# Small tasks moved among the groups of an attention pipeline, and a split moved to another PSUM bank

## The chip, the cores and the metric

The kernel runs on one core of one Trainium2 chip. The metric is the device time of one execution in microseconds (us). The engines are TensorE (PE; PEld is its weight load), VectorE (DVE), ScalarE (ACT), GpSimd (POOL) and SyncE (SP, which issues most DMAs).

## What is computed

Per batch element b (8 of them, 1024 tokens of width 256) the reference computes, with six modulation rows from a small matmul:

```python
h = _layernorm(x) * (1 + ca) + sa
x = x + ga * attention(h)          # 16 heads of 64, softmax over 1024 keys, output projection
h = _layernorm(x) * (1 + cb) + sb
x = x + gb * experts(h)            # 8 experts, each takes its 512 best tokens of all 8192
```

The experts' scores are a softmax over `h @ router_w + router_b`. Everything is float32.

## The kernel before, in words

Attention fills most of the span. Its work is cut into 128 units: one batch element, one pair of heads and one half (512) of the queries. A unit has four groups, numbered over the whole kernel by `g`; group `g` belongs to unit `g // 4`, and `g % 4` is 0, 1, 2, 3 in what the text calls its first, second, third and fourth group. 64 groups are one batch element. Nothing schedules: the order is written out by hand under `manual_schedule`, each engine executes its instructions in that order, and the framework adds the waits.

Each group, in the main loop (L727 to L763), does in this order:

- loads queued for this group (`load`);
- VectorE: subtract the row maxima (L420) from two chunks of an earlier unit (the lag is six groups);
- TensorE: two score chunks of 128 keys (L361), each into one of the two tiles "s" of the pool `ps_s` (two PSUM banks each); ScalarE copies a chunk to SBUF (L370), VectorE folds it into the running maximum `top` (L375);
- `m1` tasks: a query or key projection (`qk_task`, L326) or a value projection (`v_task`, L343), each through the one-bank tile "mm" of `ps_m`, and copied out by ScalarE;
- `post` tasks, then ScalarE: exponentials of the two subtracted chunks (L423);
- TensorE: two values products (L432); POOL adds the exponentials up (L448, L451);
- in a fourth group: `max_turn` transposes `top` into a tile "s" (L382), and `split_max` reduces it to row maxima and splits these into three bf16 parts (L390 to L398);
- `pool` tasks, then `m2` tasks.

In the next unit's first group `max_rows` transposes the parts (L404) through "mm"; in its second group `max_spread` (L417) spreads them over the partitions. The tile "mm" has one buffer, so all small tasks pass through it one after another.

The small tasks around the change are these:

- `ln_task` (L311): the norm of the next batch's inputs, two token tiles at a time: `ln_load`, `ln_stats` (VectorE, L116 and L117), `ln_norm` (POOL, L106 to L276), `ln_out`. Before, `ln_out` of every batch but the first turns by 16 ordinary matmul instructions of 64 columns (L300), and VectorE scales and shifts both halves (L305). For the first batch it turns by four transposes (L288), two for each half k of the width, and ScalarE scales and shifts a half (L291) before the next half is turned.
- `out_load`, `out_proj` (L542), `out_add`, `out_norm` (POOL, L565 to L567): the output projection of one token tile and the second norm.
- `out_turn` (L579), `out_route` (L594), `out_exp` (ScalarE, L609), `out_score` (VectorE, L616 to L620), `out_store`: the router for a pair of token tiles.

Where they stand, before, is given by `free_slot`: `ln_out`, `out_proj` and `out_turn` each take a fourth group of their own, behind the split; `out_route` takes a group that is neither a first nor a fourth. `split_max` keeps its small intermediate values in the tile "s" that it reduces:

```python
nm = tt[:, :2, :8]
```

After attention come the last batch's projection and router (L766 to L818), the choice of tokens (L876 to L952) and the experts (L1052 on).

Of the kernel before, what the change touches and what calls it, by code (L numbers as in the profile page):

```python
# [28 lines left out]
F32 = mybir.dt.float32  # L29
BF16 = mybir.dt.bfloat16  # L30
I32 = mybir.dt.int32
AF = mybir.ActivationFunctionType
ALU = mybir.AluOpType
# [4 lines left out]
P = 128  # L38
# [4 lines left out]
def adaln_block(  # L43
# [15 lines left out]
    nc = tc.nc  # L59
    B, S, D = x.shape  # L60
    H, _, _, N = w_qkv.shape
    E, _, F = w1.shape
    K = 512
    KC = D // P
    NT = S // P
# [7 lines left out]
    scale = 1.0 / N**0.5  # L73
# [4 lines left out]
    ident = const.tile([P, P], F32, name="ident")  # L78
# [17 lines left out]
    modT = const.tile([P, 2 * KC, B], F32, name="modT")  # L96
# [36 lines left out]
    ps_m = attn.enter_context(tc.tile_pool(name="ps_m", bufs=1, space=PSUM))  # L133
# [35 lines left out]
    for i in range(2):  # L169
        t = work.tile([P, NT // 2, D], F32, tag="p", name=f"x_first{i}", bufs=PB)  # L170
# [65 lines left out]
    hTs, mods, qks, vs, oTs = {}, {}, {}, {}, {}  # L236
# [4 lines left out]
    def at(g, where, f, *args):  # L241
        steps.setdefault((g, where), []).append((f, args))
# [8 lines left out]
    def bank(shape, name, start=False):  # L251

        if start:
            return ps_s.tile(shape, F32, tag="s", name=name)
        return ps_m.tile(shape, F32, tag="mm", name=name)
# [24 lines left out]
    def ln_out(b, t):  # L280
        if t == 0:
            hTs[b] = work.tile([P, KC, S], F32, tag="hT", name=f"hT{b}")
        xt = ln_x.pop((b, t))[0]
        pt = bank([P, KC, 2 * P], f"ptx{b}_{t}", (b, t) in ((0, 0), (0, 1)))
        if b == 0:
            for k in range(KC):
                for i in range(2):
                    nc.tensor.transpose(  # L288
                        pt[:, k, i * P : (i + 1) * P], xt[:, i, k * P : (k + 1) * P], ident
                    )  # L290
                nc.scalar.activation(  # L291
                    hTs[b][:, k, 2 * t * P : (2 * t + 2) * P], pt[:, k, :], AF.Identity,
                    bias=modT[:, k, b : b + 1], scale=modT[:, KC + k, b : b + 1],
                )
            return
        for k in range(KC):
            for i in range(2):
                for m in range(2):
                    c0 = k * P + m * N
                    nc.tensor.matmul(  # L300
                        pt[m * N : (m + 1) * N, k, i * P : (i + 1) * P],
                        xt[:, i, c0 : c0 + N], ident, start=True, stop=True,
                    )
        for k in range(KC):
            nc.vector.tensor_scalar(  # L305
                hTs[b][:, k, 2 * t * P : (2 * t + 2) * P], pt[:, k, :],
                modT[:, KC + k, b : b + 1], modT[:, k, b : b + 1],
                op0=ALU.mult, op1=ALU.add,
            )

    def ln_task(b, t, g):  # L311
        at(g - 4, "load", ln_load, b, t)
        at(g - 2, "post", ln_stats, b, t)
        at(g - 1, "pool", ln_norm, b, t)
        at(g, "m2", ln_out, b, t)
# [67 lines left out]
                    turned[u][:, 4 * j + t, :], top[:, j, t * P : (t + 1) * P], ident  # L383
                )

    def split_max(u):

        tt = turned.pop(u)
        nm = tt[:, :2, :8]
        nc.vector.tensor_reduce(nm[:, 0, :], tt, AX.X, ALU.max, negate=True)  # L390
        part = [
            parts_of[u % 2][:, :, :, i].rearrange("p t j -> p j t") for i in range(3)
        ]
        whole, rest = (nm[:, i, :].rearrange("p (j t) -> p j t", j=2) for i in range(2))
        nc.vector.tensor_copy(part[0], whole)
        nc.vector.tensor_sub(rest, whole, part[0])
        nc.vector.tensor_copy(part[1], rest)
        nc.vector.tensor_sub(part[2], rest, part[1])  # L398
# [171 lines left out]
    def out_turn(pool, b, t, tag="mm"):  # L570

        n = f"{b}_{t}"
        pt = pool.tile([P, 2, KC, P], F32, tag=tag, name=f"pth{n}")
        for i in range(2):
            h2 = o_h[b, t + i]
            for k in range(KC):
                for m in range(2):
                    c0 = k * P + m * N
                    nc.tensor.matmul(  # L579
                        pt[m * N : (m + 1) * N, i, k, :], h2[:, c0 : c0 + N], ident,  # L580
                        start=True, stop=True,
                    )
        h2T = small.tile([P, 2, KC, P], F32, tag="h2T", name=f"h2T{n}", bufs=1)
        nc.scalar.copy(h2T, pt)
        o_x[b, t] = h2T
# [54 lines left out]
        )  # L640


    taken = set()

    def free_slot(g, behind=False):
        while g in taken or g % 4 == 0 or behind != (g % 4 == 3):
            g += 1
        taken.add(g)
        return g


    for t in range(NT // 2):
        at(-2 if t < 2 else -1, "m1", ln_out, 0, t)
        ln_task(1, t, free_slot(39 + 4 * t, True))
    for i, g in ((0, -2), (2, -2), (1, -1), (3, 0)):
        at(g, "m1", qk_task, 0, 0, i)
    for t, g in enumerate((-1, 0, 1)):
# [1 line left out]
    for b in range(B):  # L659
        for p in range(NP):  # L660
            P0 = 8 * (b * NP + p)
            for i, g in enumerate((-7, -6, -5, -2)):
                if P0:
                    at(P0 + g, "m1", qk_task, b, p, i)
            if p % 2 == 0:
                for t, g in enumerate((-9, -3, -1, 5)):
                    if P0 or g > 0:
                        at(P0 + g, "m1", v_task, b, p // 2, t)
            if (b, p) == (B - 1, NP - 1):
                continue  # L670

            at(P0 + 17, "load", den_load, b, p)
            at(P0 + 18, "post", den_inv, b, p)
            at(P0 + 19, "load", den_spread, b, p)
            at(P0 + 20, "pool", den_mul, b, p)
        if b + 1 < B:
            if b + 2 < B:
                for t in range(NT // 2):
                    ln_task(b + 2, t, free_slot(64 * (b + 1) + 39 + 4 * t, True))
            for t in range(NT):  # L680
                g = free_slot(64 * (b + 1) + 19 + 4 * t, True)
                at(g - 2, "load", out_load, b, t)
                at(g, "m2", out_proj, ps_m, b, t)
                at(g + 1, "pool", out_norm, b, t)
                if t % 2:
                    g = free_slot(g + 2, True)
                    at(g, "m2", out_turn, ps_m, b, t - 1)
                    g = free_slot(g + 1)
                    at(g, "m2", out_route, ps_m, b, t - 1)
                    at(g + 1, "post", out_exp, b, t - 1)  # L690
                    at(g + 2, "post", out_score, b, t - 1)
                    at(g + 3, "pool", out_store, b, t - 1)
    for u in range(NSU):
        at(4 * u + 4, "m1", max_rows, u)
        if u < NSU - 1:
# [8 lines left out]
    with tc.manual_schedule():  # L704
# [21 lines left out]
        g = -2  # L726
        while g < 4 * NSU + LAG or steps:  # L727
            u, gm = divmod(g, 4)
            run(g, "load")
            if gm == 1 and 0 < u <= NSU:  # L730
                max_spread(u - 1)
            u1, gm1 = divmod(g - LAG + 1, 4)
            late = [(u1, 2 * gm1 + i) for i in range(2) if 0 <= u1 < NSU]

            for uc in late[: 1 if gm == 3 else 2]:
                subtract(*uc)
            if 0 <= u < NSU:
                for c in (2 * gm, 2 * gm + 1):
                    scores_out(u, c, scores_mm(u, c))
            if gm == 3 and late:  # L740
                subtract(*late[1])
            run(g, "m1")
            run(g, "post")
            for uc in late:
                exp_of(*uc)
            u1, gm1 = divmod(g - LAG, 4)
            if 0 <= u1 < NSU:
                for c in (2 * gm1, 2 * gm1 + 1):
                    values_mm(u1, c)
                    if u1 == NSU - 1:  # L750
                        if c == 0:
                            pd_last = ps_s.tile([P, QH], F32, tag="s", name="pd_last")
                        den_mm(pd_last, probs.pop((u1, c)), start=(c == 0), stop=(c == NT - 1))
                if gm1 == 3:
                    values_out(u1)
                if u1 < NSU - 1:
                    add_up(u1, gm1)
            if gm == 3 and 0 <= u < NSU:
                max_turn(u)
                split_max(u)  # L760
            run(g, "pool")
            run(g, "m2")
            g += 1  # L763


        b = B - 1  # L766
# [82 lines left out]
    with tc.tile_pool(name="search", bufs=2) as se, tc.tile_pool(  # L849
        name="pos", bufs=1  # L850
    ) as po_, tc.tile_pool(name="se_ps", bufs=2, space=PSUM) as sps, tc.tile_pool(
        name="pos_ps", bufs=1, space=PSUM
    ) as pps:
        for dst, pattern, mult in (
# [3 lines left out]
            i = po_.tile(list(dst.shape), I32, name=f"i_{dst.name}")  # L858
# [29 lines left out]
        for s in range(15):  # L888
            bit = 28 - 2 * s
            cnt = se.tile([P, 3], F32, tag="cnt", name=f"cnt{s}")  # L890
            for k in range(3):
# [3 lines left out]
                    op0=ALU.is_ge, op1=ALU.add, accum_out=cnt[:, k : k + 1],  # L895
# [209 lines left out]
```

## Time and profile before

| | us |
|---|---|
| median of three runs | 3621.32 |
| lowest, highest run | 3620.8, 3622.61 |
| the profiled execution | 3623.01 |
| span of its trace | 3621.3 |

| line and engine | what | count | busy us | mean ns |
|---|---|---|---|---|
| L451 POOL | adding up exponentials | 762 | 1806.3 | 2370 |
| L420 DVE | subtracting maxima | 1024 | 1206.5 | 1209 |
| L423 ACT | exponentials | 1024 | 1041.8 | 1057 |
| L361 PE | scores | 4096 | 1024.6 | 612 |
| L432 PE | values product | 4096 | 968.2 | 593 |
| L382 PE | turn of the maxima | 1024 | 139.9 | 280 |
| L579 PE | router's turn | 512 | 39.1 | 296 |
| L300 PE | norms' turn | 448 | 30.6 | 279 |
| L305 DVE | scale and shift of the norms | 56 | 27.7 | 536 |
| L291 ACT | the same, first batch | 8 | 4.4 | 562 |

Busy time is the union of a group's intervals. A float32 matmul of the program stands in the trace as two instructions, a transpose as one. Matmuls overlap, so what a piece of TensorE's work takes of its chain is read from the start of its first matmul to the start of the next piece, not from the means.

### The profile page before, as it was taken

To read this page: it belongs to the slowest core of one execution; us is meant where nothing else is said; L and a number is where in the kernel's file an instruction comes from. 1 tells how busy PE (TensorE), PEld (TensorE's weight loads), DVE (VectorE), ACT (ScalarE), POOL (GpSimd) and SP (SyncE) were. 2 spreads that over 40 slices of the span, in tenths; PEclk is the share of its full clock that TensorE was granted. 3 is DMA by queue.
4 is the path that set the end of the run, shared out by engine and by line. 5 is a ranking of instruction groups with operands and counts; after the bars stand their busy time and mean duration, and the time that the engine had idled before them with its cause. 6 is when DMAs were issued, how large, how long until landed. Compare 5 with 4: busy or idle time off the path is not lost. (4 is left out here: it accounts for less than half of the span.)

```text
span 3621.3 us, 54202 instructions
## 1 busy us (share of the span) xinstructions
PE 3462.3 (96%) x20622; PEld 1457.6 (40%) x20622; DVE 2898.7 (80%) x3641; ACT 2436.6 (67%) x2988; POOL 2658.8 (73%) x1537
## 2 busy tenths in 40 slices
PE   7999999999999999999999999999999999982898
PEld 3333333343433443344433434334334344342565
DVE  4889888888888888888888888888888888857442
ACT  4777777777777777777777777777777777730111
POOL 1778778888788877977788788877788877851232
PEclk9999999999999999999999999999999999995999
DMA  4021013011121112111211112011301121133332
GB/s 77 13 42 31 25 32 66 30 45 45 58 52 35 49 52 64 31 39 51 58 48 44 40 44 62 30 52 48 67 29 45 45 59 48 51 87 121 94 100 41
DMA packets 189652, 185.39 MB, mean 51 GB/s; under 512 B 48952, under 2 KB 167240, under 8 KB 189264
## 3 DMA queue, kind: packets, MB, share of 16 engines
q1 hardware_dynamic: 170448, 159.50, 16.1%
q0 software_dynamic: 7168, 12.72, 1.7%
q10 hardware_dynamic: 11776, 9.71, 0.9%
q8 instruction: 162, 2.65, 0.3%
q14 instruction: 98, 0.80, 0.1%
HBM read 127.06 MB, written 63.21 MB: 53 GB/s over the span
## 5 line engine op out<-in xcount | busy, mean ns | idle before, releaser
L451 POOL TENSOR_TENSOR acc<-acc,p 128x1024 f32<-128x1024 f32 x762 | 1806.3, 2370 | 361.3 <-ACT p L423 328.2
L370 ACT COPY p<-s 128x1024 f32<-128x1024 f32 x1024 | 996.1, 1018 | 417.8 <-PE s L361 407.5
L420 DVE TENSOR_TENSOR p<-p,less 128x1024 f32<-128x1024 f32 x1024 | 1206.5, 1209 | 33.0 <-PE less L417 30.4
L375 DVE TENSOR_TENSOR top<-top,s 128x1024 f32<-128x1024 f32 x768 | 936.6, 1220 | 266.9 <-ACT p L370 226.6
L423 ACT ACTIVATE p<-p 128x1024 f32<-128x1024 f32 x1024 | 1041.8, 1057 | 73.8 <-DVE p L420 73.4
L361 PE MATMUL s<-qk,qk 64*128 64x512 f32 x4096 | 1024.6, 612 | 33.4 <-DVE parts L398 31.0
L432 PE MATMUL av<-p,v 128*64 128x512 f32 x4096 | 968.2, 593 | 1.8 <-ACT oT L441 1.8
L361 PEld LDWEIGHTS s<-qk,qk 64*128 64x128 f32 x4096 | 358.6, 186 | 525.6 <-issue 240.1
L326 PE MATMUL pq<-hT,wq 128*64 128x512 f32 x2048 | 498.7, 608 | 1.3 <-ACT v L348 0.7
L432 PEld LDWEIGHTS av<-p,v 128*64 128x64 f32 x4096 | 280.8, 137 | 461.8 <-issue 366.2
L448 POOL TENSOR_TENSOR acc<-p,p 128x1024 f32<-128x1024 f32 x127 | 301.7, 2376 | 183.3 <-ACT p L423 183.3
L326 PEld LDWEIGHTS pq<-hT,wq 128*64 128x64 f32 x2048 | 124.8, 136 | 341.8 <-issue 212.6
L343 PE MATMUL pv<-wq,hT 128*64 128x256 f32 x2048 | 251.0, 387 | 1.4 <-ACT qk L331 0.7
L1030 ACT ACTIVATE h<-ph,b_sb 128x512 f32<-128x512 f32 x64 | 44.0, 687 | 275.9 <-PE ph L1026 275.9
L390 DVE TENSOR_REDUCE tt<-tt 128x8 f32<-128x1024 f32 x128 | 157.4, 1230 | 68.3 <-PE tt L382 68.2
L542 PE MATMUL po<-wo,ot 128*64 128x256 f32 x1792 | 205.7, 382 | 0.0
L343 PEld LDWEIGHTS pv<-wq,hT 128*64 128x64 f32 x2048 | 136.3, 137 | 155.6 <-issue 66.3
L375 DVE TENSOR_TENSOR top<-p,s 128x1024 f32<-128x1024 f32 x128 | 155.7, 1217 | 29.9 <-ACT p L370 29.9
L382 PEld LDWEIGHTS tt<-ident,top 128*128 128x128 f32 x1024 | 109.6, 140 | 107.4 <-DVE top L375 107.4
L513 POOL TENSOR_TENSOR oT<-oT,rb 128x1024 f32<-128x1024 f32 x63 | 149.9, 2379 | 3.2 <-DMA rb<-rden_d 3.2
L542 PEld LDWEIGHTS po<-wo,ot 128*64 128x64 f32 x1792 | 123.5, 137 | 66.2 <-issue 9.4
L382 PE MATMUL tt<-ident,top 128*128 128x128 f32 x1024 | 139.9, 280 | 3.3 <-DVE top L375 3.3
(166 smaller groups left out, 2356.5 us busy)
## 6 DMA issues: line engine op xcount, KB each, us to landing
rb<-rden_d SPq DMA_DIRECT2D x128, 256.0 KB
oT_d<-oT SPq DMA_DIRECT2D x62, 512.0 KB
ot<-oT_d SPq DMA_DIRECT2D x56, 512.0 KB
rows_d<-row SPq DMA_DIRECT2D x64, 132.0 KB
rows_d<-gb_d SPq DMA_DIRECT2D x8, 1024.0 KB
w<-in_L_ffn_w_dram ACTq DMA_DIRECT2D x8, 1024.0 KB
w<-in_L_ffn_w_dram SPq DMA_DIRECT2D x8, 1024.0 KB
lnx<-in_L_attn_inputs_dram SPq DMA_DIRECT2D x28, 256.0 KB
```

The lines of the kernel that those rows point to most:

```text
L326: nc.tensor.matmul(pq[m * N : (m + 1) * N, :], wq_of(k, a, 2 * p + m), hTs[b][:, k, sl], start=(k == 0), stop=(k == KC - 1),)
L343: nc.tensor.matmul(pv[m * N : (m + 1) * N, i, :], hTs[b][:, k, t0 : t0 + N], wq_of(k, 2, 4 * g, 4), start=(k == 0), stop=(k == KC - 1),)
L361: nc.tensor.matmul(ps[:, j, :], kt[r, c * P : (c + 1) * P], qt[r, h * QB : (h + 1) * QB], start=True, stop=True,)
L370: nc.scalar.copy(probs[u, c], ps)
L375: nc.vector.tensor_tensor(tops[u], probs[u, 0] if c == 1 else tops[u], ps, ALU.max)
L382: nc.tensor.transpose(turned[u][:, 4 * j + t, :], top[:, j, t * P : (t + 1) * P], ident)
L420: nc.vector.tensor_tensor(probs[u, c], probs[u, c], less[u], ALU.add)
L423: nc.scalar.activation(probs[u, c], probs[u, c], AF.Exp)
L432: nc.tensor.matmul(avs[u][j * N : (j + 1) * N, :], v[:, c, hh * N : (hh + 1) * N], pT[:, j, :], start=(c == 0), stop=(c == NT - 1),)
L448: nc.gpsimd.tensor_tensor(sums[u], pts[0], pts[1], ALU.add)
L451: nc.gpsimd.tensor_tensor(sums[u], sums[u], pt, ALU.add)
L542: nc.tensor.matmul(po[m * N : (m + 1) * N, :], ot[:, p, m * N : (m + 1) * N], wo[:, p, :], start=(p == 0), stop=(p == NP - 1),)
```

## The change

It does four things. `ln_out` uses the first batch's form for all batches: transposes over the whole 128 x 128 array, and ScalarE for the output, half by half. `out_turn` uses transposes over the whole array as well. `split_max` gets a flag: where a projection follows in the same group, it works in the tile "s" as before, elsewhere in a tile "mm". And `free_slot` is gone: the norms' turns for batch b + 1 stand in the third groups of the first four units of batch b (groups 2, 6, 10, 14 of its 64; before, in its fourth groups 39, 43, 47, 51); the projections stand in fourth groups 19, 23, 31, 35, 43, 47, 55, 59 of the next batch's 64; the router's turn three groups after the second projection of a pair, which is a third group, its matmul six groups after, its exponentials, scores and stores seven, eight and nine groups after.

```diff
     def ln_out(b, t):
...
-        if b == 0:
-            for k in range(KC):
-                for i in range(2):
-                    nc.tensor.transpose(
-                        pt[:, k, i * P : (i + 1) * P], xt[:, i, k * P : (k + 1) * P], ident
-                    )
-                nc.scalar.activation(
-                    hTs[b][:, k, 2 * t * P : (2 * t + 2) * P], pt[:, k, :], AF.Identity,
-                    bias=modT[:, k, b : b + 1], scale=modT[:, KC + k, b : b + 1],
-                )
-            return
         for k in range(KC):
             for i in range(2):
-                for m in range(2):
-                    c0 = k * P + m * N
-                    nc.tensor.matmul(
-                        pt[m * N : (m + 1) * N, k, i * P : (i + 1) * P],
-                        xt[:, i, c0 : c0 + N], ident, start=True, stop=True,
-                    )
-        for k in range(KC):
-            nc.vector.tensor_scalar(
-                hTs[b][:, k, 2 * t * P : (2 * t + 2) * P], pt[:, k, :],
-                modT[:, KC + k, b : b + 1], modT[:, k, b : b + 1],
-                op0=ALU.mult, op1=ALU.add,
+                nc.tensor.transpose(
+                    pt[:, k, i * P : (i + 1) * P], xt[:, i, k * P : (k + 1) * P], ident
+                )
+            nc.scalar.activation(
+                hTs[b][:, k, 2 * t * P : (2 * t + 2) * P], pt[:, k, :], AF.Identity,
+                bias=modT[:, k, b : b + 1], scale=modT[:, KC + k, b : b + 1],
             )
...
-    def split_max(u):
+    def split_max(u, busy):
 
         tt = turned.pop(u)
-        nm = tt[:, :2, :8]
+
+        nm = tt[:, :2, :8] if busy else ps_m.tile([P, 2, 8], F32, tag="mm", name=f"nm{u}")
...
     def out_turn(pool, b, t, tag="mm"):
...
-                for m in range(2):
-                    c0 = k * P + m * N
-                    nc.tensor.matmul(
-                        pt[m * N : (m + 1) * N, i, k, :], h2[:, c0 : c0 + N], ident,
-                        start=True, stop=True,
-                    )
+                nc.tensor.transpose(pt[:, i, k, :], h2[:, k * P : (k + 1) * P], ident)
...
-    taken = set()
-
-    def free_slot(g, behind=False):
-        while g in taken or g % 4 == 0 or behind != (g % 4 == 3):
-            g += 1
-        taken.add(g)
-        return g
+
+    covered = set()
...
-        ln_task(1, t, free_slot(39 + 4 * t, True))
...
-            if b + 2 < B:
-                for t in range(NT // 2):
-                    ln_task(b + 2, t, free_slot(64 * (b + 1) + 39 + 4 * t, True))
+            for t in range(NT // 2):
+                ln_task(b + 1, t, 64 * b + 2 + 4 * t)
             for t in range(NT):
-                g = free_slot(64 * (b + 1) + 19 + 4 * t, True)
+                g = 64 * (b + 1) + 19 + 4 * (t + t // 2)
+                covered.add(g)
                 at(g - 2, "load", out_load, b, t)
                 at(g, "m2", out_proj, ps_m, b, t)
                 at(g + 1, "pool", out_norm, b, t)
                 if t % 2:
-                    g = free_slot(g + 2, True)
-                    at(g, "m2", out_turn, ps_m, b, t - 1)
-                    g = free_slot(g + 1)
-                    at(g, "m2", out_route, ps_m, b, t - 1)
-                    at(g + 1, "post", out_exp, b, t - 1)
-                    at(g + 2, "post", out_score, b, t - 1)
-                    at(g + 3, "pool", out_store, b, t - 1)
+                    at(g + 3, "m2", out_turn, ps_m, b, t - 1)
+                    at(g + 6, "m2", out_route, ps_m, b, t - 1)
+                    at(g + 7, "post", out_exp, b, t - 1)
+                    at(g + 8, "post", out_score, b, t - 1)
+                    at(g + 9, "pool", out_store, b, t - 1)
...
             if gm == 3 and 0 <= u < NSU:
                 max_turn(u)
-                split_max(u)
+                split_max(u, g in covered)
```

## The prediction

> **What bounds the kernel now.** I read the page first, then the waits, then the timeline of single units.
>
> ```profile
> PE 3462.3 (96%) x20622; PEld 1457.6 (40%) x20622; DVE 2898.7 (80%) x3641; ACT 2436.6 (67%) x2988; POOL 2658.8 (73%) x1537
> ```
>
> TensorE is busy for 96% of the span, the next engine for 80%. A busy TensorE proves little by itself, so I measured from the start of one piece of its work to the start of the next over all 512 groups. The pieces repeat to 0.01 us: two score chunks 1.91, a query/key task 1.77, a value task 1.78, a values product 1.82, a projection (L542) 3.60, the turn of the maxima (L382) 1.02, a turn of 16 small matmuls (L300, L579) 1.02. In the stretches between 36 and 3,200 us the clock column reads 1.00. So attention is one TensorE chain, and a microsecond put on it is a microsecond of time. Its only regular wait is in the waits view:
>
> ```profile
> PE s L361 <- DVE parts L398: 31.0, 70, 1.3
> ```
>
> Seventy of 128 units wait at their end. The timeline of a unit without small work at its end (columns: start, duration, engine, line, operation, tiles, idle before it):
>
> ```profile
> 83.08 1.09 PE L382 MATMUL tt<-ident,top 128*128 128x128 f32 x8
> ...
> 84.10 1.13 PE L361 MATMUL s<-qk,qk 64*128 64x512 f32 x4
> 84.21 1.23 DVE L390 TENSOR_REDUCE tt<-tt 128x8 f32<-128x1024 f32 x1 [0.74 <-PE tt L382]
> ...
> 86.14 0.19 DVE L398 TENSOR_TENSOR parts<-tt,parts 128x8 bf16<-128x8 f32 x1
> ...
> 86.48 1.13 PE L361 MATMUL s<-qk,qk 64*128 64x512 f32 x4 [1.25 <-DVE parts L398]
> 87.54 0.41 PE L404 MATMUL pn<-ident_b,parts 128*64 128x128 bf16 x8
> ```
>
> Let T be the start of L382 (83.08). The reduction ends at T+2.36, the split at T+3.25, and only 0.15 later, at T+3.40, does the second score chunk start, because the split works inside the score bank that this chunk needs. The row turn L404 starts at T+4.46. Now a unit with a turn of the next batch's norms at its end (T = 1106.22):
>
> ```profile
> 1107.24 1.09 PE L300 MATMUL ptx<-ident,lnx 128*64 128x128 f32 x16
> ...
> 1109.62 1.13 PE L361 MATMUL s<-qk,qk 64*128 64x512 f32 x4 [0.22 <-DVE parts L398]
> ...
> 1110.68 0.41 PE L404 MATMUL pn<-ident_b,parts 128*64 128x128 bf16 x8
> ```
>
> Again L404 starts at T+4.46: the 1.02 us turn lies wholly inside a wait that would be there anyway. That holds for all 28 turns L300 and all 27 turns L579 that are followed by a unit. With a projection there, L404 starts at T+6.54 and nothing waits.
>
> **What the change is worth, part by part.** The built order of the changed kernel leaves all 56 projections at units' ends, where the split stays in the score bank: nothing changes there, since the projection covers it (split done by T+5.03 at the latest, second chunk at T+5.59). The other 70 inner units (15 + 28 + 27) end with nothing.
>
> *Split in the small bank.* The second chunk now waits for the reduction: T+2.36 + 0.15 = T+2.51, and L404 follows 1.06 later at T+3.57 (the split's end plus 0.15, T+3.40, is earlier). Gain 4.46 - 3.57 = 0.89 per unit. No trace shows this release; its bounds are no gain (the split still holds the bank) and 1.06 (only the split's end holds L404). I take 0.89, from the row of the reduction that the built order names as what the chunk waits for. The small bank's last reader before it is a ScalarE copy that ended at 1105.20, 2.1 us before the reduction starts: no new wait. In six units it goes otherwise: the score operations of a batch's last pair (L616 to L620) now fall in a fourth group without a projection (the first units of batches 2 to 7, counted from 0). They push the reduction from T+1.13 to T+2.52 wherever they stand now, always under a projection. There the chunk starts at T+3.90 and L404 at T+4.96: 0.50 worse. Sum: -64 x 0.89 + 6 x 0.50 = **-54.0**.
>
> *Turns over the whole array, in third groups.* They now stand on the chain. Starts within L382 are 0.166 and then 0.109 apart, and 0.205 passes from the last to the next mode's matmul, so four transposes cost 0.166 + 2 x 0.109 + 0.205 = 0.59, against 1.02 for 16 matmuls. The router's turn (out_turn, all four, then one copy) costs that: 27 x 0.59 = **+15.9** (bounds 0.59 and the present 1.02). POOL ended its rows 9.2 us after the projection's start and the turn comes 19 us after it, so no wait.
>
> [...]
>
> *The next batch's norms.* Here the code, not the size, matters. The two halves (k) share one tile; ScalarE reads the first half before the second is turned, and the built order makes the second half's transposes wait for that ScalarE instruction. The first batch does so already, at the start of the trace:
>
> ```profile
> 24.65 0.44 PE L288 MATMUL ptx<-ident,x_first 128*128 128x128 f32 x2
> ...
> 25.26 0.56 ACT L291 ACTIVATE hT<-ptx,modT 128x256 f32<-128x256 f32 x1
> ...
> 25.88 0.44 PE L288 MATMUL ptx<-ident,x_first 128*128 128x128 f32 x2 [0.79 <-ACT hT L291]
> 26.35 0.56 ACT L291 ACTIVATE hT<-ptx,modT 128x256 f32<-128x256 f32 x1 [0.53 <-PE ptx L288]
> ```
>
> Half to half takes 1.22 us with an idle ScalarE. In a third group ScalarE is not idle. Such a group, from 1095.21:
>
> ```profile
> 1099.60 1.99 ACT L423 ACTIVATE p<-p 128x1024 f32<-128x1024 f32 x2
> ...
> 1100.71 1.99 PE L361 MATMUL s<-qk,qk 64*128 64x512 f32 x8
> ```
>
> Its values product ends 5.50 us after the group's start (1100.71), where the turn will be; the exponentials, queued ahead, end at 6.38. ScalarE overlaps successive instructions by 0.1, so the first half's output runs 6.28 to 6.84, the second half's transposes start 0.05 later at 6.90, and the next scores at 6.90 + 0.166 + 0.205 = 7.27. Queued behind the waiting transposes on TensorE is everything: the scores and all after. So such a turn costs 7.27 - 5.50 = 1.77, not 0.59. In five of them out_exp (L609) stands ahead of the exponentials and moves them by 0.38 (849.36 in a group that starts at 844.59): 2.15. Bounds: 0.59 (no wait) and 2.15 everywhere; the rows favour 1.77. 22 x 1.77 + 5 x 2.15 = **+49.7**. The second half's ScalarE output ends near 7.95, before copy 6 can start (7.27 + 1.23). VectorE loses 56 x 0.54 (L305), which covered nothing. The statistics (1.08) move to first groups, where by the rows VectorE ends the maximum that frees the sixth chunk's bank at T+12.49 for a start at T+12.80. POOL's norm, now behind two additions, ends some 9.7 us after its second group's start; the turn comes at 10.9. SP issues the loads two groups before the statistics, as now.
>
> [...]
>
> *Start.* The first turn comes in group 2, in the bank that the mod row then uses: 1.22 + 0.48 + 0.56 + 0.06 = 2.32. In group 3 the second mod row waits for the split to leave that bank: T+3.40 instead of T+1.02, 2.38. The statistics in group 4 delay a maximum that scores wait for there (0.39 idle already): 1.1. **+5.8** (bounds 0 and 8). *End.* After attention the last turn is shorter: **-0.5**; the one at group 510 stands where TensorE waits anyway.
>
> Sum: -54.0 + 15.9 + 49.7 + 5.8 - 0.5 = **+16.9**. The profiled execution took 3623.0 (span 3621.3 and 1.7 around it), which gives 3639.9; the median of the runs is 1.7 lower, so I predict 3638.
>
> **Rivals.** *A, the halves don't wait* (the other side). If the second half's transposes ran while ScalarE reads the first, the norms would cost 0.59 each: 22 x 1.18 + 5 x 1.56 + 1.7 at the start = 35.5 less, 3603. It turns where such a turn costs 1.14 (1.77 less 16.9/27). For it: different columns. Against: the idle 0.79 above, five times over. 0.08. *B, VectorE or ScalarE becomes late.* The slacks after the shortened wait are 0.18 (sixth chunk's bank), 0.26 (denominators' bank behind the row copy) and 0.5 (last maximum before L382). If one is missed by 0.3 in 28 to 70 units: +8 to +21, 3646 to 3659. For it: VectorE runs without a gap from the reduction to the third group. Against: each engine's rows repeat to 0.01. 0.12. *C, the split still holds the score bank*: no gain of 0.89, 3638 + 57 = 3695. Against: the built wait. 0.03.
>
> **How the numbers follow.** Forecast 0.77, its own range 3630 to 3647 (0.1 off the 0.89 is 6, 0.15 off the 1.77 is 4, the start 3); A 0.08, B 0.12, C 0.03. Range 3628 to 3650: it leaves out A, C and half of B. The ends of the bounds that lie outside it are A and C themselves. A measurement can tell 0.2% (7 us). Faster by more: 0.08 (A). Within: 0.05 (forecast and A mixed). Slower: 0.87.
>
> **What would show it.** Right: norm turns with two transposes, a gap of about 1 us ended by ScalarE, two more; L404 at T+3.57 in 64 units and near T+4.96 in six; router turns without a wait. Wrong: norm turns in one piece (A), score chunks in second groups idle behind VectorE's maxima (B), second chunks ended by L383 where no projection stands (C).

## The result, and the profile after

The changed kernel takes 3637.91 us (median of six runs, 3636.95 to 3639.0); the kernel before, measured beside it, 3621.29 (six runs, 3620.69 to 3623.46). The ratio is 1.0048, 95% interval 1.0039 to 1.0058: slower by 0.5%. The profiled execution took 3638.05, its span 3636.0; before, 3623.01 and 3621.3. So the profiles differ by 15.0 where the sum of the prediction gave 16.9.

The busy times of the page of after (all lines of after from here on have new numbers: L345 scores, L366 the turn of the maxima, L375 to L383 the split, L389 the row turn, L287 and L290 the norms' turn and output):

```profile
PE 3440.8 (95%) x19902; PEld 1427.0 (39%) x19902; DVE 2867.6 (79%) x3585; ACT 2465.4 (68%) x3044; POOL 2659.9 (73%) x1537
```

TensorE, the engine that sets the time, is busy for 21.5 us less than before, and the kernel is 15 us longer. Busy time alone would have called this a gain. The waits of TensorE (engine, tile and line; what was waited for; total, times, longest) say where the rest is:

```profile
PE ptx L287 <- ACT hT L290: 36.4, 33, 5.1
PE s L345 <- DVE nm L375: 31.3, 70, 1.6
```

The second line is the one that the split had before, now on the reduction L375 instead of the split's last step L398; 70 waits still, with almost the same total. Of the first, before had five waits at the start of the trace (7.9 us); the other 28 are new, and 27 of them, 28 us, stand in third groups. Here is one of its waits, in a third group that starts at 450.17, and behind it the unit's end (timeline of after; start, duration, engine, line, operation, tiles, idle before it):

```profile
453.85 1.89 PE L417 MATMUL av<-p,v 128*64 128x512 f32 x8
...
454.56 2.00 ACT L408 ACTIVATE p<-p 128x1024 f32<-128x1024 f32 x2
...
455.67 0.44 PE L287 MATMUL ptx<-ident,lnx 128*128 128x128 f32 x2
456.46 0.56 ACT L290 ACTIVATE hT<-ptx,modT 128x256 f32<-128x256 f32 x1
...
457.07 0.44 PE L287 MATMUL ptx<-ident,lnx 128*128 128x128 f32 x2 [0.96 <-ACT hT L290]
...
457.43 1.99 PE L345 MATMUL s<-qk,qk 64*128 64x512 f32 x8
457.54 0.57 ACT L290 ACTIVATE hT<-ptx,modT 128x256 f32<-128x256 f32 x1 [0.53 <-PE ptx L287]
...
462.95 1.09 PE L366 MATMUL tt<-ident,top 128*128 128x128 f32 x8
...
463.97 1.13 PE L345 MATMUL s<-qk,qk 64*128 64x512 f32 x4
464.15 1.23 DVE L375 TENSOR_REDUCE nm<-tt 128x8 f32<-128x1024 f32 x1 [0.76 <-PE tt L366]
...
465.43 1.13 PE L345 MATMUL s<-qk,qk 64*128 64x512 f32 x4 [0.34 <-DVE nm L375]
...
466.49 0.41 PE L389 MATMUL pn<-ident_b,parts 128*64 128x128 bf16 x8
```

The turn takes 457.43 - 455.67 = 1.76 us of TensorE's chain. Its first two transposes are done early; ScalarE is still in the exponentials (454.56 to 456.56), then reads the first half (456.46 to 457.02), and only 0.05 later do the other two transposes start. At the unit's end the opposite: with T = 462.95 the second score chunk starts at T+2.48 and the row turn at T+3.54, where before they started at T+3.40 and T+4.46.

In the first units of batches 2 to 7 the same wait is longer. One of them, T = 838.86:

```profile
838.86 1.09 PE L366 MATMUL tt<-ident,top 128*128 128x128 f32 x8
...
839.63 1.83 DVE L600 TENSOR_SCALAR row<-ex,rd 128x8 f32<-128x8 f32 x2
...
841.37 1.22 DVE L375 TENSOR_REDUCE nm<-tt 128x8 f32<-128x1024 f32 x1
...
842.65 1.13 PE L345 MATMUL s<-qk,qk 64*128 64x512 f32 x4 [1.64 <-DVE nm L375]
...
843.71 0.41 PE L389 MATMUL pn<-ident_b,parts 128*64 128x128 bf16 x8
```

VectorE does the last pair's scores (L600 here) ahead of the reduction, which so starts at T+2.51 instead of T+1.20. L389 comes at T+4.85.

Counted from the same group in both traces, after is behind before by 4.25 us at group 128, 8.05 at 192, 11.86 at 256, 15.67 at 320, 19.47 at 384: 3.8 per batch element. That is what one batch's pieces make: three turns of 1.77 and one of 2.15, four router turns of 0.59, seven gains of 0.91 and one loss of 0.40 (the split's two cases) sum to +3.85. In the last batch, which has no norms to turn, it gets 7 us back.

### The profile page after: what moved, and what is told of

Read it like the earlier page. It is cut to its first block, busy times and chain, and to the rows that moved or that the text cites. A ratio compares the mean times of both kernels' runs of the same rounds, so it can differ in the third digit from the quotient of the medians.

```text
span 3636.0 us, 52807 instructions
## 1 busy us (share of the span) xinstructions
PE 3440.8 (95%) x19902; PEld 1427.0 (39%) x19902; DVE 2867.6 (79%) x3585; ACT 2465.4 (68%) x3044; POOL 2659.9 (73%) x1537
## 5 line engine op out<-in xcount | busy, mean ns | idle before, releaser
L345 PE MATMUL s<-qk,qk 64*128 64x512 f32 x4096 | 1025.1, 613 | 34.2 <-DVE nm L375 31.3
L345 PEld LDWEIGHTS s<-qk,qk 64*128 64x128 f32 x4096 | 356.3, 186 | 493.4 <-issue 198.9
L366 PEld LDWEIGHTS tt<-ident,top 128*128 128x128 f32 x1024 | 109.6, 140 | 107.8 <-DVE top L359 107.8
L366 PE MATMUL tt<-ident,top 128*128 128x128 f32 x1024 | 139.9, 280 | 3.7 <-DVE top L359 3.7
L332 ACT COPY v<-pv 128x512 f32<-128x512 f32 x128 | 75.1, 587 | 99.7 <-PE pv L327 99.7
```

The lines of the kernel that those rows point to most:

```text
L345: nc.tensor.matmul(ps[:, j, :], kt[r, c * P : (c + 1) * P], qt[r, h * QB : (h + 1) * QB], start=True, stop=True,)
L366: nc.tensor.transpose(turned[u][:, 4 * j + t, :], top[:, j, t * P : (t + 1) * P], ident)
```

## The experiments

Each kernel below is after with the edit shown, but for the sixth. They were measured in two sets, 1 to 4 and 5 to 7, each with the kernel before beside them: 3620.14 (seven runs) in the first, 3619.81 (thirteen) in the second, and the ratios are to these. "Attention" is read from the traces: from the first score matmul to the last turn of the maxima. It leaves out the start, whose length differs between kernels (the first scores come at 30.8 to 36.7 us), and the stretch behind attention (423.9 to 429.2).

| kernel | median | ratio to before, 95% | attention |
|---|---|---|---|
| before | 3621.29 | | 3157.84 |
| after | 3637.91 | 1.0048 (1.0039 to 1.0058) | 3173.86 |
| 1 both halves turned first | 3599.38 | 0.9941 (0.9925 to 0.9958) | 3141.65 |
| 2 split in the score bank | 3703.44 | 1.0227 (1.0210 to 1.0244) | 3242.11 |
| 3 router's turn in columns | 3645.84 | 1.0069 (1.0052 to 1.0086) | 3183.70 |
| 4 split in SBUF | 3933.58 | 1.0867 (1.0849 to 1.0885) | 3466.84 |
| 5 = 1, and the last scores moved | 3591.86 | 0.9921 (0.9905 to 0.9938) | 3132.68 |
| 6 before, with whole-array turns | 3619.29 | 0.9999 (0.9989 to 1.0009) | 3157.60 |
| 7 = 1, outputs on VectorE | 3598.93 | 0.9946 (0.9929 to 0.9962) | 3139.49 |

The theory is the prediction's: the chain of TensorE lengthens by each turn that stands in a third group, the norms' turns cost three times what their transposes cost because ScalarE reads one half before the other is turned, and the early release of the score bank gives back 0.9 us a unit.

### 1. All four transposes ahead of the outputs

```diff
             for i in range(2):
                 nc.tensor.transpose(
                     pt[:, k, i * P : (i + 1) * P], xt[:, i, k * P : (k + 1) * P], ident
                 )
+        for k in range(KC):
             nc.scalar.activation(
```

> In the norms' turn all four transposes are issued before the two ScalarE outputs (also for the first batch, at the start). Theory (the second half's transposes wait for ScalarE's read of the first half, 1.77 us per turn instead of 0.59): 22 x 1.18 + 5 x 1.56 = 33.8 less, some 0.4 less at the first turn in group 2 and up to 3 less before attention, so 3601 to 3605; each turn L287 takes 0.59 from its first transpose to the next scores. Rival (the price is that of transposes between two other modes in a third group, whatever waits): unchanged, 3638.

Measured: 3599.38, 0.6% under before and just under the expected range. A turn of the same batch as in the timeline above, one unit earlier, in this kernel:

```profile
422.08 2.01 ACT L409 ACTIVATE p<-p 128x1024 f32<-128x1024 f32 x2
...
423.20 0.66 PE L287 MATMUL ptx<-ident,lnx 128*128 128x128 f32 x4
...
423.78 1.99 PE L346 MATMUL s<-qk,qk 64*128 64x512 f32 x8
423.99 1.01 ACT L291 ACTIVATE hT<-ptx,modT 128x256 f32<-128x256 f32 x2
```

Four transposes in one piece, 0.58 us, and the scores follow at once, while ScalarE still finishes the exponentials and takes both outputs behind them: nobody waits for it. All 27 turns are like this (0.58 to 0.59). That makes 22 x 1.18 + 5 x 1.56 = 33.8 less, and 0.4 at the first turn; attention became 32.2 shorter. The difference is the clock of TensorE. In the first unit the task that makes the second modulation row (L218) starts after the same wait in both kernels, here in kernel 1 and then in after:

```profile
60.08 3.57 PE L218 MATMUL pr<-wm,sT 128*8 128x512 f32 x4 [2.33 <-issue]
66.69 1.88 PE L218 MATMUL pr<-wm,sT 128*8 128x512 f32 x4 [2.33 <-issue]
```

In kernel 1 the granted clock is 0.50 from 58.67 us on for 6.8 us, in after it stays at 1.00. From this task to the row turn that takes 6.35 us instead of 3.72, 2.6 more; without it attention would be 34.8 shorter. The rest of the gain came ahead of attention, whose first scores now start at 30.84 instead of 36.71: there too each turn waited for a half. The expectation had up to 3 us for that. The clock goes with the rest: before, after and kernels 4 and 6 have 6.8 us at 0.50 shortly ahead of the first scores, which come at 36.1 to 36.7; kernels 2 and 3 have 3.4 us of it and begin at 34.5 and 34.9; kernels 1, 5 and 7, with both halves turned first, have none there and begin at 30.8 to 32.0. One inserted line turns the change from a loss into a gain: the wait inside the turn is what made it slower.

In after the second half's transposes waited 0.96 us for the reader of the first, though the two halves lie in different columns of the tile. Kernel 1 keeps the tile as it is: it puts the readers behind the last writer, and the wait has nothing left to hold.

### 2. The split back in the score bank

```diff
-                split_max(u, g in covered)
+                split_max(u, True)
```

> The split always works in the score bank, the rest of the changed kernel as it is. Theory (the second score chunk then waits for the split's end again): L404 at 4.46 us after L366 in 64 units instead of 3.55, and at 5.84 instead of 4.86 in the six with the score operations: 64 x 0.91 + 6 x 0.98 = 64.1 more, 2.4 less at the start where the second mod row no longer waits for the split: 3699 to 3701. Rival (the earlier release is hidden by the rest of the pipeline): about 3638.

Measured: 3703.44; the span is 66.5 longer than after's, attention 68.3. L389 is at T+4.46 in 64 units again, against 3.55: 64 x 0.91 = 58.2. The six late units show something that the expectation had not (timeline of kernel 2):

```profile
1263.95 1.09 PE L366 MATMUL tt<-ident,top 128*128 128x128 f32 x8
1264.97 1.13 PE L345 MATMUL s<-qk,qk 64*128 64x512 f32 x4
1268.72 2.08 PE L345 MATMUL s<-qk,qk 64*128 64x512 f32 x4 [2.62 <-DVE parts L383]
1270.73 0.64 PE L389 MATMUL pn<-ident_b,parts 128*64 128x128 bf16 x8
1271.16 3.63 PE L417 MATMUL av<-p,v 128*64 128x512 f32 x8
```

The wait is 2.62 instead of 1.64 (6 x 0.98 = 5.9), and behind it the same work takes about twice as long: a score chunk 2.08 instead of 1.13, a values product 3.63 instead of 1.89. The clock is why (windows of kernel 2; start and end, length, then busy time and instructions of PE, PEld, DVE, ACT, POOL, the granted clock, share and GB/s of DMA):

```profile
1270.00:1271.00 1.00, 1.00 (x8) 0.27 (x8) 0.81 (x1) 0.10 (x1) 1.00 (x1) 0.50 0.00 0
1271.00:1272.00 1.00, 1.00 (x10) 0.40 (x8) 0.06 (x1) 1.00 (x2) 0.38 (x1) 0.50 0.00 0
```

The granted clock reads 0.50. From L389 to the next scores it is 2.86 us as a rule; four of the six late units show 3.3 to 4.9 there, 4.9 more in all, and the slow chunk ahead of L389 adds 2.8. At the start 2.4 are saved, as expected, because the second modulation row no longer waits for the split. 58.2 + 5.9 + 4.9 + 2.8 - 2.4 = 69.4, measured 68.3. After's waits of 1.64 left the clock at 1.00 in the unit shown above, from 843 us on.

### 3. The router's turn again by 16 matmuls of 64 columns

```diff
-                nc.tensor.transpose(pt[:, i, k, :], h2[:, k * P : (k + 1) * P], ident)
+                for m in range(2):
+                    c0 = k * P + m * N
+                    nc.tensor.matmul(
+                        pt[m * N : (m + 1) * N, i, k, :], h2[:, c0 : c0 + N], ident,
+                        start=True, stop=True,
+                    )
```

> The router's turn goes back to 16 matmuls of 64 columns, in its new third group. Theory (a turn in a third group stands on TensorE's chain at its own price): the mode of the values product before it stays, so 1.02 less 0.10 for the switch against 0.59: 27 x 0.33 = 9 more, 3647. Rival (the array's form does not matter, since the third group has slack): 3638.

Measured: attention 9.8 longer than after's. A turn takes 0.97 instead of 0.59, but the values product ahead of it 1.72 instead of 1.82: both use the 64-column tiling, and the change of tiling, 0.10, falls between other pieces. 27 x (0.38 - 0.10) = 7.6. The other 2.2 are the clock's again: after the wait of 2.33 in the first unit it falls to 0.50 for 6.8 us, and from L218 to the row turn pass 6.41 us instead of after's 3.72, 2.7 more. So the whole-array form does what it is for, by 7 to 8 us, where the turn stands on the chain. The intervals of the two ratios overlap; the pieces tell the two kernels apart.

### 4. The split's small values in SBUF

```diff
-        nm = tt[:, :2, :8] if busy else ps_m.tile([P, 2, 8], F32, tag="mm", name=f"nm{u}")
+        nm = tt[:, :2, :8] if busy else small.tile([P, 2, 8], F32, tag="lg", name=f"nm{u}")
```

> Where no projection stands the split's intermediate values lie in SBUF, not in the small bank. Theory (the small bank costs nothing but the 2.4 us of the second mod row at the start): 3635 to 3636, L404 still 3.55 us after L366. Rival (VectorE's casts from SBUF are held up while POOL adds, as the router's L600 multiplication is, 1.72 us beside a POOL addition): the split ends 1.5 to 2 us later, L404 waits for it, 70 x 1.4 to 1.8 more: 3730 to 3765.

Measured: 296 us more than after. The rival held, and its price was far too low. The groups of the split's two middle steps (line, engine, operation, tiles; count; busy time, mean ns; idle before) in kernel 4:

```profile
L381 DVE TENSOR_TENSOR nm<-nm,parts 128x8 f32<-128x8 f32 x72 | 147.6, 2050 | 2.5
L382 DVE CAST parts<-nm 128x8 bf16<-128x8 f32 x72 | 86.4, 1200 | 2.5
```

They are the same steps on 8 elements that take 175 and 194 ns from PSUM in after. One case (timeline of kernel 4):

```profile
168.23 2.35 POOL L436 TENSOR_TENSOR acc<-acc,p 128x1024 f32<-128x1024 f32 x1
168.32 2.28 DVE L381 TENSOR_TENSOR nm<-nm,parts 128x8 f32<-128x8 f32 x1
...
170.53 2.34 POOL L498 TENSOR_TENSOR oT<-oT,rb 128x1024 f32<-128x1024 f32 x1
170.64 2.28 DVE L382 CAST parts<-nm 128x8 bf16<-128x8 f32 x1
...
172.95 0.19 DVE L383 TENSOR_TENSOR parts<-nm,parts 128x8 bf16<-128x8 f32 x1
...
173.20 0.39 PE L389 MATMUL pn<-ident_b,parts 128*64 128x128 bf16 x4 [3.95 <-DVE parts L383]
```

Each of the two starts just after a POOL instruction of 2.35 us has started, and ends with it. So it goes throughout: L381 is long (2.3) in 64 of these 72 uses and L382 in 35, all 99 end within 0.12 us of the end of a POOL instruction, and of the 45 short ones (0.2) 44 ran beside no such instruction. What lets such an instruction of VectorE begin with POOL's and end with it, no run here shows. The second chunk is not touched (it waits for L375, as in after), but L389 is: it idles 1.85 us in 36 units, 3.95 in 28 and 2.83 in six, 194.2 in all (200.0 in the waits view, with the last unit, behind attention). The other 100 us are the clock again (windows of kernel 4, behind the wait above):

```profile
174.00:175.00 1.00, 1.00 (x4) 0.24 (x2) 1.00 (x2) 1.00 (x2) 0.00 (x0) 0.50 0.98 401
175.00:176.00 1.00, 1.00 (x4) 0.24 (x2) 1.00 (x2) 0.97 (x2) 0.47 (x1) 0.50 0.01 0
176.00:177.00 1.00, 1.00 (x8) 0.05 (x8) 0.51 (x1) 0.47 (x1) 1.00 (x1) 0.66 0.00 0
177.00:178.00 1.00, 1.00 (x14) 0.50 (x14) 0.00 (x0) 0.35 (x1) 0.92 (x2) 1.00 0.00 0
```

Half speed for 3.4 us from the end of the wait on. From L389 to the next scores it is 2.85 without a wait, 4.97 on average after 3.95, 4.49 after 2.83, 3.73 after 1.85: 28 x 2.12 + 6 x 1.64 + 36 x 0.88 = 101. So the small bank is not an incidental place for the split: in SBUF, beside this much POOL work, its values cost far more than the bank does.

### 5. The last pair's scores moved to a group with a projection

```diff
-                    at(g + 8, "post", out_score, b, t - 1)
-                    at(g + 9, "pool", out_store, b, t - 1)
+                    g += 24 if t == NT - 1 and b + 2 < B else 8
+                    at(g, "post", out_score, b, t - 1)
+                    at(g + 1, "pool", out_store, b, t - 1)
```

This stands on top of kernel 1.

> The kernel of e1_halves_together, and the score operations (L617 to L621) of a batch's last pair moved 16 groups on, under the next batch's first projection; their store follows one group after. Theory (in six units they hold up the reduction and L404 stands at 4.86 instead of 3.55 us): 6 x 1.31 = 7.9 less than e1_halves_together, 3591 to 3592, L404 at 3.55 in all 70 units without a projection. Rival (VectorE catches up later in those units anyway, so the 1.31 is made good): 3599.

Measured: 3591.86, and attention 9.0 shorter than kernel 1's. Of that 1.2 is the clock: after the same wait of 2.33 it falls for 3.4 us here and for 6.8 in kernel 1 (5.20 against 6.35 from L218 to the row turn). The other 7.8 are the expected 7.9. The wait for the reduction (waits of kernel 5):

```profile
PE s L346 <- DVE nm L376: 23.5, 70, 0.3
```

Still 70 waits, but the longest is 0.3 instead of 1.6, and the row turn starts at T+3.55 in all 70 units. This is the fastest kernel of the study: 0.8% under before, 1.3% under after.

### 6. The whole-array turns alone, nothing moved

The kernel before, with transposes in `out_turn` and in `ln_out`; the norms' outputs stay on VectorE, behind all four transposes. The diff shows `ln_out`; `out_turn` is changed likewise:

```diff
             for i in range(2):
-                for m in range(2):
-                    c0 = k * P + m * N
-                    nc.tensor.matmul(
-                        pt[m * N : (m + 1) * N, k, i * P : (i + 1) * P],
-                        xt[:, i, c0 : c0 + N], ident, start=True, stop=True,
-                    )
+                nc.tensor.transpose(
+                    pt[:, k, i * P : (i + 1) * P], xt[:, i, k * P : (k + 1) * P], ident
+                )
...
```

> The kernel before, with whole-array transposes in out_turn and in ln_out (all four ahead of VectorE's outputs) and nothing moved: the turns stay in fourth groups, the split in the score bank. Theory (there a turn lies inside the wait for the split, so its length is worth nothing): L404 4.46 us after L382 as before, 3619 to 3620, 0.5 to 1 less after attention. Rival (a shorter turn shortens the unit): 55 x 0.43 to 0.58 less, 3588 to 3596.

Measured: no difference (ratio 0.9989 to 1.0009, ten runs). A unit's end with a turn, T = 1105.87 (timeline of kernel 6), and the wait in the waits view:

```profile
1105.87 1.09 PE L379 MATMUL tt<-ident,top 128*128 128x128 f32 x8
...
1106.80 0.60 PE L298 MATMUL ptx<-ident,lnx 128*128 128x128 f32 x4
...
1107.33 1.13 PE L358 MATMUL s<-qk,qk 64*128 64x512 f32 x4
...
1109.27 1.13 PE L358 MATMUL s<-qk,qk 64*128 64x512 f32 x4 [0.81 <-DVE parts L395]
...
1110.33 0.41 PE L401 MATMUL pn<-ident_b,parts 128*64 128x128 bf16 x8
```

```profile
PE s L358 <- DVE parts L395: 63.3, 70, 1.3
```

The turn is 0.53 us instead of 1.02, the turn of the maxima ahead of it 0.93 instead of 1.02, and the second chunk starts at T+3.40 and the row turn at T+4.46 all the same. The wait for the split has grown from 31.0 to 63.3, by 55 x 0.59: where TensorE's turns became 0.58 shorter, its idle time became as much longer. So the turns were hidden where they stood, as the prediction read it from single units, and speeding them up there is worth nothing.

### 7. Outputs by VectorE, behind all four transposes

```diff
-            nc.scalar.activation(
-                hTs[b][:, k, 2 * t * P : (2 * t + 2) * P], pt[:, k, :], AF.Identity,
-                bias=modT[:, k, b : b + 1], scale=modT[:, KC + k, b : b + 1],
+        for k in range(KC):
+            nc.vector.tensor_scalar(
+                hTs[b][:, k, 2 * t * P : (2 * t + 2) * P], pt[:, k, :],
+                modT[:, KC + k, b : b + 1], modT[:, k, b : b + 1],
+                op0=ALU.mult, op1=ALU.add,
             )
```

> The kernel of e1_halves_together with the two outputs of the norms' turn on VectorE (L291, for the first batch too), 0.54 us each. Theory (the wait came from the order of halves, not from the engine; VectorE has 1 us to spare in a third group before the next copy): 3597 to 3603, turns L287 at 0.59. Rival (ScalarE's room is what the change needed, VectorE's 0.99 us per turn makes the maxima late): 27 x 0.5 to 1 more than e1_halves_together, 3613 to 3626.

Measured: 3598.93, the same as kernel 1 within the intervals, with turns of 0.58 to 0.59. Its attention is 2.2 shorter than kernel 1's, but its clock did not fall in the first unit, which is worth 2.6. So the cost of the changed norms was the order of the halves and not the engine that puts them out.

## Why the prediction was right, step by step

| step | predicted | measured |
|---|---|---|
| split in the small bank, 64 units | L389 at T+3.57: -0.89 each | T+3.55: -0.91 each |
| the six late units | T+4.96: +0.50 each | T+4.86: +0.40 each |
| sum of both | -54.0 | -55.8 |
| router's turns | 27 x 0.59 = +15.9 | 0.58 to 0.59 each |
| norms' turns | 22 x 1.77 + 5 x 2.15 = +49.7 | 1.76 to 1.77 and 2.15 each |
| start | +5.8 | 5.7 up to group 8 |
| end | -0.5 | -1.4 behind the last group |
| total | +16.9 | 14.1 by these rows, 15.0 by the profiled executions |

**The step that carried it** was to price a norm turn by the instruction order and not by the size of its transposes. With 0.59 for them the sum would have been a gain of some 19 us, the rival A. Kernel 1 is that rival made real, by another order, and it lies at 3599. The two parts of the 1.77 are both seen in the timeline above: the exponentials queued ahead on ScalarE, and the half-to-half wait. How much each would cost alone was not tried; the start, where ScalarE is idle, had 1.22 from half to half. The argument against the rival took the idle 0.79 there as seen five times over; four of the five waits are 0.66 to 0.79, the other is 5.1. The mechanism was the right one all the same.

**The gain of the split** rested on no row of before, only on the reading that the second chunk would wait for the reduction. It came out within 0.02, by two errors that cancel: the reduction starts at T+1.20, not T+1.13 (with the scratch in SBUF, kernel 4, it is back at T+1.13, so the small bank adds the 0.07), and the chunk follows its end by 0.05, not 0.15. That much is luck. Kernel 2 gives the term back.

**That before's turns cost nothing** was read from L404 at T+4.46 with and without them. Kernel 6 shows it from the other side.

**Rival B** (VectorE or ScalarE late) did not come: behind the first units TensorE's regular waits in attention are the two lines shown, and the total is below the forecast, not above. **Rival C** did not either: the second chunks name L375. The start and the end are small; the start was right in sum, though its first turn took 2.16 for 2.32 predicted. That the forecast of 3638 lies 0.1 from the median is luck too: the runs spread over 2 us, and the rows add up to 14.1 where 16.9 was forecast.

What stays open: how the 1.77 divides into its two parts, half a microsecond to one in the sums of kernels 1, 2 and 3, and why two slots of the clock (3.413 us each) that were idle for 58 and 59% (the first units of after and kernel 7) were not followed by half speed. The clock was no term of the prediction; between before and after it made no difference within attention, where both traces read 1.00 from 37.4 us on.

## What to carry to other kernels

Price a moved instruction at the place it moves to: the same turn cost nothing inside a wait, 0.59 us on the chain and 1.77 on the chain with a reader between its halves. Where several writes fill one PSUM tile, issue all of them before the first reader, or the writing engine takes on the reader's queue (1.77 us a turn here, and 0.58 with the readers behind); and where a tile is scratch as well as result, give the scratch another bank, so that the next writer waits for one reader only (0.91 us in each of 64 units). A wait of 1.85 us cost 1.7 more where the clock fell behind it (kernel 4). A change that is slower as a whole can hold a gain: undoing it part by part found a version 1.3% under it.

## What the runs showed of the hardware that was not expected

- **The clock fell behind waits of 1.85 to 3.95 us, but not behind all, and two of equal length differed.** Half speed followed all 28 waits of 3.95 us and all six of 2.83 in kernel 4, but also four of six waits of 2.62 (kernel 2), 19 of 36 of 1.85 (kernel 4; the stretch from L389 to the next scores is 4.4 to 4.6 there, in the other 17 at most 2.9), and the wait of 2.33 in the first unit in kernels 1, 3 and 5, not in after and 7. In each of the nine traces all changes of the granted clock lie whole multiples of 3.413 us apart (in before half speed from 30.06 to 36.89 us and from 3204.46 to 3207.87, in after from 30.56 to 37.39 and from 3215.20 to 3218.61), and where this row of slots of 3.413 us begins differs from trace to trace (by 0.50 between these two). Two equal waits of 2.62 in kernel 2 show the difference (windows, cut at the slots; columns as above):

```profile
1264.77:1268.18 3.41, 1.33 (x7) 0.34 (x5) 3.31 (x6) 1.74 (x2) 3.33 (x2) 1.00 0.23 78
1268.18:1271.60 3.42, 2.88 (x14) 1.20 (x16) 2.60 (x4) 0.70 (x1) 3.20 (x4) 0.50 0.01 2
2087.38:2090.80 3.42, 1.66 (x10) 0.67 (x8) 3.32 (x6) 2.07 (x2) 3.34 (x2) 1.00 0.14 47
2090.80:2094.21 3.41, 2.55 (x18) 1.00 (x20) 3.13 (x7) 1.33 (x2) 3.41 (x4) 1.00 0.09 32
```

The first wait leaves 2.08 us of one slot idle (61%), and the clock falls at that slot's end; the second is cut by a slot's end and leaves 1.76 (51%) in one and 0.86 in the next, and it stays. From 40 us to the end of attention the nine traces hold 8,327 slots that ran at 1.00. In 66 of them TensorE was idle for 54% or more: 60 were followed by half speed, for one slot or two (all 38 from 60% idle on). Of the other 8,261 none was. The ends of matmuls are modelled, so the 54% is rough. A wait of 1.85 that was followed by half speed cost 1.7 more behind it.

- **Eight elements took 2.28 us.** A subtraction and a cast of 128 x 8 with their operands in SBUF ended only with a POOL instruction of 2.35 us, where the same two from PSUM took 0.18 and 0.19 (kernel 4 and after).
- **A change of tiling took about 0.10 us** on TensorE: the values product measured 1.82 when a whole-array turn followed (after) and 1.72 when a turn of the same 64-column tiling did (kernel 3).
